# Both ends of a gated state-space convolution kernel rewritten on one core: opening by channel halves, first and last six pairs reordered, no clip

## The chip, the cores and the metric

The kernel runs on one core of a Trainium2 chip. A core has a matrix engine (TensorE, "PE" in the profile, with "PEld" for its weight loads), a vector engine (VectorE, "DVE"), an activation engine (ScalarE, "ACT"), a general engine (GpSimd, "POOL") and a sequencer that only issues transfers here (SyncE, "SP"). Each works through its own instruction list in order and waits on semaphores. The metric is the time of one execution in device microseconds (us); lower is better.

## What is computed

The input x has shape (4, 128, 96, 96). It is group-normalised (32 groups), read as a sequence of 9216 positions in four directions (rows, columns, and both reversed), and each direction runs through the same block:

```python
t = grouped1x1(x, in_proj)                  # 128 -> 512 channels, 4 groups
u, gate = t[:, :256], t[:, 256:]
u = depthwise_conv5(silu(u))
s = ssm_in(u); a = 0.999 + 0.0009 * sigmoid(ssm_delta(u))
a = clip(a, 0.0001, 0.9999)
bb, cc = tanh(ssm_b(u)), tanh(ssm_c(u))     # 32 channels each
h[l] = a[l] * h[l-1] + bb[l] * s[l]         # written as cumsum in the reference
u = u + ssm_out(cc * h + d * s)
y = out_proj(grouped1x1(u * sigmoid(gate), mix))
```

The four results are mixed by a 1x1 convolution (fuse) and added to x. The clip's upper end is the value that `a` has where the sigmoid is 1, so it never moves `a` by more than rounding.

## The kernel before, in words

All arithmetic is float32. A *unit* is one direction of one block of 384 positions; two opposite directions make a *pair*. There are 8 phases (4 images, columns then rows), 6 steps in a phase, 4 pairs in a step: 192 pairs, numbered t = 0 to 191. `R` = 4 sub-sequences, `LAG` = 6.

`pair(t)` (line 762) writes the order of all five engines out by hand (line 916, `manual_schedule`): what stands first in the source is issued first on its engine. In one call it does, for pair t, the depthwise convolution and the projections, and for pair t-6 the rest:

- `front(t+4)` (413, 466): in-projection by 32x32 matmuls out of `x_in`, then four silu on ACT (480) into the tile `sil`. Only in the first three steps of a phase; the others reload `sil` from device memory.
- `conv` and `conv_less` (587, 596): the lower 128 channels' taps as matmuls with the banded weights `band` and `less`; ACT copies the sum to `u` (606, 608). `taps` (613): the upper 128 channels' five taps, the first on ACT (623, `first_tap`), four on DVE (625).
- `proj` (637): 16 matmuls with `main`, then on ACT tanh, copy, tanh (654 to 656), on POOL the decay `a` and its clip (659; for the second and third pair of a step the clip is DVE's, 789) and the product of bb and s (662).
- `scan` (685): two DVE scans for each step, in the first two pairs of the next one. `outputs` (700): two POOL products and a POOL copy for each pair, which make z; `scale_s` (677, 679) on ACT.
- `gates_and_out` or, where gates were kept, `out_of` (494, 497): matmuls from z into the banks 0 to 3, over a copy of u put there by ACT (`under`, 502, 505); `gating` (563, 574) on DVE; `accumulate` (715): 16 matmuls with `w_fin` for each unit, an ACT copy `ys` (727, 729), a POOL add to the image `acc` (743).

PSUM has eight banks. Banks 0 to 3 serve `out_of`, `under` and the taps; in the first six pairs `conv` and `proj` both use banks 4 and 5 (`PROJ`, 120) and `front` 7, 6, 2, 3 (`FRONT`). Transfers are all on SP's queue, in the order of the source: `load_front` (249) fetches `x_in` for a later step as soon as a front has read its part, `keep_silu` (453) writes 770 KB of `sil` to device memory, `load_chunks` (390) fetches pieces of the next image for its statistics.

Ahead of the pairs, not hand ordered: x is loaded and its statistics taken on DVE (281), weights are merged (351 to 369), POOL builds `band` and `less` with 64 scalings of 32 columns (343), and `stats_finish` (175) turns the statistics into scaled weights `wn` (225) and biases `bnorm` (238). The weight-merging tiles lie in a pool that is closed at line 370; `sil` takes over its memory. `fronts` for the first four groups follow (909 to 914).

Behind the pairs, `tail` (869): for the six pairs still open (186 to 191) `out_of`, `gating`, `under`, two scans, `outputs`, `accumulate`, one pair after the other, and the last four transfers of 384 KB to the result.

Of the kernel before, what the change touches and what calls it, by code (L numbers as in the profile page):

```python
# [52 lines left out]
DMIN, DMAX = 0.999, 0.9999  # L53
PAD = K // 2
# [12 lines left out]
def conv_preact_kernel(  # L67
# [214 lines left out]

    b0 = phases[0][0]
    first_table = wp.tile([P, 1], F32, name="first_table")
# [50 lines left out]
    for s in range(2):  # L335
        for p in range(R):
            for k in range(2):
                r, to = slice(0, P), band[:, s, p]
                if k == less_of(p):
                    r, to = less_rows(s, p), less[:, p]  # L340
                for g in range(4):
                    m = R * k - p + R - 1
                    nc.gpsimd.tensor_scalar_mul(  # L343
                        to[r, g, :], id32[r, :], w_dw[r, s, g, m : m + 1]
                    )
# [23 lines left out]
    nc.scalar.activation(b_fin, pb[:, 0:1], AF.Identity, bias=b_fuse)  # L369
    prep.__exit__(None, None, None)  # L370
# [46 lines left out]
    def front_parts(i, banks):  # L417

        step, g = divmod(i, R)
        if step * UB >= NU:  # L420
            return
        st = step % NS
        if st == NS // 2:
            sils[step] = sils[step - 1]
            load_silu(step + 1, (g,))
        elif st == NS - 1 and g < 2:
            load_silu(step, (2 * g, 2 * g + 1))
        elif g == 0 and fresh(step):
            sils[step] = wk.tile([P, 2, 2, 4, N + 1], F32, tag="sil", name=f"sil_{step}")
        if fresh(step):  # L430
            yield from compute_front(step, g, banks)
        sil = sils[step]

        if st == 0:
            engine = nc.gpsimd if step else nc.vector
            for s in range(2):
                engine.memset(sil[64 * s : 64 * s + 64, s, 0, g, 0:1], 0.0)
            if g < 2:
                engine.memset(sil[:, :, 1, g, 0:1], 0.0)

        for s in range(2):
            load_front(step + 1, s, slice(64 * s + 32, 64 * s + 64), slice(g, g + 1))
        if g == R - 1:
            for s in range(2):
                load_front(step + 1, s, slice(64 * s, 64 * s + 32), slice(0, R))
        if st < NS // 2 - 1:
            to_keep.append((step, g))
        if step > 1:
            keep_silu(1)
# [15 lines left out]

    def compute_front(step, g, banks):
        un = units[step * UB]
        wn, bn = stats[un["b"]]
        sil = sils[step]
        for s in range(2):  # L470
            for j in range(2):
                r = slice(64 * s + 32 * j, 64 * s + 32 * j + 32)
                for c in range(4):
                    m, q = (c, g) if j else (g, R - 1 - c if s else c)
                    mm(bank(banks[2 * s + j]), c, wn[r, s, 32 * m : 32 * m + 32],
                       x_in[s][r, q, :], True, True)
        yield
        for s in range(2):
            for j in range(2):
                nc.scalar.activation(  # L480
                    sil[:, s, j, g, :],
                    bank(banks[2 * s + j])[:, : N + 1],
                    AF.Silu,
                    bias=bn[:, 1:2] if j else bn[:, 4 + g : 5 + g],
                )
# [47 lines left out]
    def load_last():  # L533

        t = wk.tile([P, 2, 2, 4, N + 1], F32, tag="sil", name="last_gates")
        for e in range(R):
            n = NU // 2 - R + e
            old_gates[n] = t[:, :, :, e, :N]
            nc.sync.dma_start(old_gates[n], kept[n // NP % 2][mirror(n)])
# [97 lines left out]
    def proj(i, banks, apart=False):  # L637

        step, p = units[i]["step"], units[i]["p"]
        if step not in scans:  # L640
            t0 = wk.tile([P, N, R], F32, tag="t0", name=f"t0_{step}")
            scans[step] = t0.rearrange("p n r -> p r n")
        ta = scans[step]
        tb = tbs[i] = wk.tile([P, N], F32, tag="t1", bufs=LAG + 1, name=f"t1_{units[i]['id']}")

        turns = [(e, j) for j in (1, 0) for e in range(2)]
        for e, j in sorted(turns) if apart else turns:
            for c, cols in enumerate(((qb, qb, qa, qa), (qs, qs, qc, qc))[e]):
                first, end = (j == 0, j == 1) if apart else (j == 1, j == 0)
                mm(bank(banks[e]), c, w_proj[:, j, cols], us[i][:, c % 2, j, :], first, end)  # L650
        pa, pb = (bank(bk)[:, :N] for bk in banks)

        tm = tms[i] = wk.tile([P, N], F32, tag="tm", name=f"tm_{units[i]['id']}")
        nc.scalar.activation(tm, pa, AF.Tanh, bias=b_proj[:, 0:1])  # L654
        nc.scalar.copy(tb[0:64, :], pb[0:64, :])
        nc.scalar.activation(tb[64:P, :], pb[64:P, :], AF.Tanh, bias=b_proj[64:P, 1:2])  # L656
        for op in decay(i):
            if i < NU - 2:
                nc.gpsimd.tensor_scalar(*op)  # L659
            if clip_late(i):  # L660
                break
        nc.gpsimd.tensor_mul(ta[0:64, p, :], tb[0:64, :], tm[0:64, :])  # L662

    def decay(i):

        a = scans[units[i]["step"]][64:P, units[i]["p"], :]
        half = (DMAX - DMIN) / 2
        return (
            (a, tms[i][64:P, :], half, DMIN + half, ALU.mult, ALU.add),
            (a, a, 0.9999, 0.0001, ALU.min, ALU.max),  # L670
        )

    def clip_late(i):

        return units[i]["p"] in (1, 2)
# [24 lines left out]
    def outputs(i, copy=nc.gpsimd.tensor_copy):  # L700
        ta, tb, p = scans[units[i]["step"]], tbs[i], units[i]["p"]
        nc.gpsimd.tensor_mul(ta[0:64, p, :], tb[64:P, :], ta[64:P, p, :])  # L702
        nc.gpsimd.tensor_add(tb[0:64, :], ta[0:64, p, :], tb[0:64, :])  # L703
        copy(tb[64:P, :], tb[0:64, :])
# [10 lines left out]
    def accumulate(bu, bk, adder=nc.gpsimd, last=False):  # L715

        b, s, p, st = bu["b"], bu["s"], bu["p"], bu["st"]
        py = bank(bk)
        for j in range(2):
# [4 lines left out]
        if not (last and s == 1):  # L724
# [17 lines left out]
        def add():  # L742
            adder.tensor_add(part, y, part)  # L743
# [17 lines left out]

    def pair(t):
# [5 lines left out]
        with_front = fresh((t + R) // R)  # L768
        seed = old or back and not with_front

        ahead = old or back and not with_front
        banks, w = plan(with_front or not back)
        if back:
            front(t + R, FRONT)
# [5 lines left out]
        send()  # L780
# [5 lines left out]
        new_u(i)  # L786
        taps(i, range(1, K))
        if t and clip_late(i - 2):
            nc.vector.tensor_scalar(*decay(i - 2)[1])
        conv(i, banks)  # L790
        if not ahead:
            conv_less(i, banks)
        if not back:
            first_tap(i + 2)
            front(t + R, FRONT)
# [14 lines left out]
        if waiting and not late:  # L810
            accumulate(waiting.pop(0), w[0])()
# [6 lines left out]
        if ahead:  # L818
            accumulate(waiting.pop(0), w[1])()
# [33 lines left out]
        proj(i, PROJ, between)  # L853
# [7 lines left out]
        if t == NU // 2 - 3:  # L861
            load_last()
# [6 lines left out]
    def tail():  # L869

        first, banks = NU // 2 - LAG, (6, 7, 4, 5)

        for op in decay(NU - 2):
            nc.vector.tensor_scalar(*op)
        scale_s(NU - 2)
        outputs(2 * first + 2)
        last = None
        for n in range(first, NU // 2):
            i = 2 * n
            for s in range(2):  # L880
                for j in range(2):
                    out_of(i, s, j)
            for s in range(2):
                gating(i, s)
                if i + 2 < NU:
                    under(i + 2, s)
            if n == first:
                for part in range(2):
                    scan(NU // UB - 1, part)

            if last:
                last()
            if i + 4 < NU:
                outputs(i + 4, lambda *_: None)
            accumulate(waiting.pop(0), banks[2])()
            last = accumulate(waiting.pop(0), banks[3], nc.vector)
            if i + 4 < NU:
                nc.scalar.copy(tbs[i + 4][64:P, :], tbs[i + 4][0:64, :])
            send()
            waiting.extend(units[i : i + 2])  # L900
        last()
        for s in range(2):
            accumulate(waiting.pop(0), banks[2 + s], nc.vector, True)()
            send()

    pieces = stats_finish(b0)
    for _ in range(4):
        next(pieces)
    fronts = [front_parts(i, [4 * (i % 2) + e for e in range(4)]) for i in range(R)]
    next(fronts[0])  # L910
    next(pieces, None)
    for parts in fronts:
        for _ in parts:
            pass
    taps(0, range(1))
    with tc.manual_schedule(
# [3 lines left out]
    ):  # L920
        for t in range(NU // 2):
# [81 lines left out]
```

## Time and profile before

| what | value |
|---|---|
| median of 4 runs (lowest to highest) | 1841.81 us (1840.99 to 1843.59) |
| the profiled execution: its own time | 1842.24 us |
| the profiled execution: its span | 1840.5 us |
| busy: PE, ACT, POOL, DVE | 1806.4, 1567.8, 1564.5, 1546.0 us |
| PE busy in 0 to 100 us | 81.20 of 100 us |
| PE busy in 100 to 1775 us | 1669.15 of 1675 us |
| PE busy in 1803.4 to 1840.5 us | 28.12 of 37.1 us |

The profile is a record of one execution: the page sums it up, and the trace behind it can be asked for a stretch of time. In a timeline row the numbers are start, duration, engine, line, operation, output and inputs, shape, count, and in brackets the idle time ahead of it and what ended that. In a row of windows they are, for a stretch of time, the busy time of PE, PEld, DVE, ACT and POOL with instruction counts, the share of full speed that TensorE's clock was granted, the share of time in which the transfer engines worked, and GB/s. One `matmul` of the source is two PE instructions in the count (32 rows x384 are 16 calls).

### The profile page before, as it was taken

How to read it: one execution, taken by the hardware profiler on the slowest of the kernel's cores; microseconds unless marked ns; L12 is line 12 of the kernel's file. 1: busy time of each engine (PE TensorE's matmuls, PEld its weight loads, DVE VectorE, ACT ScalarE, POOL GpSimd, SP SyncE). 2: the span in 40 equal slices, each digit the busy share in tenths (PEclk: the TensorE clock that was granted, in tenths of full speed). 3: DMA queues.
4: the chain of work that ended last, by engine and by line, in shares of the span. 5: the costliest groups of instructions: out<-in, count | busy, mean ns of one | idle time of the engine just before them, and what ended most of it. 6: DMA issues, size and time to landing. Idle time of an engine off the chain costs nothing.

```text
span 1840.5 us, 57440 instructions
## 1 busy us (share of the span) xinstructions
PE 1806.4 (98%) x24024; PEld 650.9 (35%) x24024; DVE 1546.0 (84%) x1541; ACT 1567.8 (85%) x2773; POOL 1564.5 (85%) x1615
## 2 busy tenths in 40 slices
PE   6999999999999999999999999999999999999998
PEld 3233333333333333333333333333333333333332
DVE  5889888888888988988888998888888888788886
ACT  4888888988888888898888888888888888888975
POOL 5489998889878999888887999888888789998886
PEclk7999999999999999999999999999999999999999
DMA  6755464543975467344695556543477634645434
GB/s 195 193 195 179 130 203 118 172 143 130 290 245 177 160 186 212 101 144 139 197 304 202 167 170 197 147 143 117 159 227 230 234 126 136 205 108 177 148 108 168
DMA packets 147826, 321.18 MB, mean 175 GB/s; under 512 B 14192, under 2 KB 115696, under 8 KB 147568
## 3 DMA queue, kind: packets, MB, share of 16 engines
q1 hardware_dynamic: 147136, 316.56, 54.0%
q8 instruction: 189, 3.10, 0.7%
q10 hardware_dynamic: 432, 0.96, 0.1%
q14 instruction: 69, 0.57, 0.1%
HBM read 185.21 MB, written 132.25 MB: 172 GB/s over the span
## 4 chain that ended last, share of the span: by engine, by line
PE 92%; ACT 3%; POOL 2%; issue 1%; DVE 1%; POOLq 0%; DVEq 0%; ACTq 0%
PE psum L133 79%; PE psum L497 8%; PE psum L491 5%; ACT sil L480 1%; ACT psum L623 0%; POOL acc L743 0%; ACT u L606 0%; POOL t L659 0%; POOL t L702 0%; POOL t L703 0%; ACT t L656 0%; ACT tm L654 0%; POOL t L662 0%; ACT t L679 0%; DVE u L574 0%
## 5 line engine op out<-in xcount | busy, mean ns | idle before, releaser
L625 DVE SCALAR_TENSOR_TENSOR psum<-sil,small,psum 128x768 f32<-128x768 f32 x576 | 589.1, 1023 | 35.6 <-ACT psum L623 9.5
L133 PE MATMUL psum<-u,w_fin 128*32 128x384 f32 x6144 | 551.9, 489 | 0.0
L133 PE MATMUL psum<-u,main 128*32 128x384 f32 x6144 | 534.9, 489 | 0.0
L574 DVE SCALAR_TENSOR_TENSOR u<-gate,psum 128x768 f32<-128x768 f32 x376 | 349.6, 952 | 166.9 <-ACT gate L514 85.0
L743 POOL TENSOR_TENSOR acc<-ys,acc 128x384 f32<-128x384 f32 x376 | 414.5, 1123 | 23.8 <-ACT ys L729 5.8
L702 POOL TENSOR_TENSOR t<-t,t 64x384 f32<-64x384 f32 x192 | 256.1, 1334 | 86.6 <-DVE t L696 49.0
L133 PEld LDWEIGHTS psum<-u,w_fin 128*32 128x32 f32 x6144 | 188.1, 110 | 321.0 <-issue 219.1
L133 PEld LDWEIGHTS psum<-u,main 128*32 128x32 f32 x6144 | 181.7, 110 | 326.0 <-issue 199.4
L133 PE MATMUL psum<-sil,band 128*32 128x384 f32 x3072 | 288.8, 491 | 8.1 <-ACT ys L729 3.1
L703 POOL TENSOR_TENSOR t<-t,t 64x384 f32<-64x384 f32 x192 | 283.9, 1478 | 15.1
L505 ACT COPY psum<-u 128x768 f32<-128x768 f32 x352 | 276.8, 800 | 13.0 <-DVE u L625 9.0
L659 POOL TENSOR_SCALAR t<-tm 64x384 f32<-64x384 f32 x191 | 177.7, 930 | 98.3 <-ACT tm L654 68.7
L497 PE MATMUL psum<-t,main 32*128 32x384 f32 x1536 | 241.0, 513 | 3.9 <-POOL t L703 1.5
L623 ACT ACTIVATE psum<-sil,small 128x768 f32<-128x768 f32 x192 | 174.1, 907 | 63.3 <-DVE u L574 56.3
L514 ACT ACTIVATE gate<-psum,bnorm 128x384 f32<-128x384 f32 x384 | 192.6, 581 | 28.8 <-PE psum L491 26.3
L662 POOL TENSOR_TENSOR t<-t,tm 64x384 f32<-64x384 f32 x192 | 201.6, 1050 | 15.3
L625 DVE SCALAR_TENSOR_TENSOR u<-sil,small,psum 128x768 f32<-128x768 f32 x192 | 194.9, 1015 | 7.8
L480 ACT ACTIVATE sil<-psum,bnorm 128x385 f32<-128x385 f32 x384 | 191.6, 584 | 5.5 <-POOL band L343 3.4
L133 PE MATMUL psum<-sil,less 64*32 64x384 f32 x3072 | 168.7, 496 | 0.0
L491 PE MATMUL psum<-x_in,wn 32*128 32x384 f32 x768 | 162.3, 528 | 2.4 <-ACT u L606 1.2
L729 ACT COPY ys<-psum 128x384 f32<-128x384 f32 x287 | 132.9, 476 | 31.0 <-PE psum L133 29.1
L133 PEld LDWEIGHTS psum<-sil,band 128*32 128x32 f32 x3072 | 89.2, 109 | 184.1 <-issue 89.6
(87 smaller groups left out, 1664.3 us busy)
## 6 DMA issues: line engine op xcount, KB each, us to landing
sil<-sil SPq DMA_DIRECT2D x128, 770.0 KB, 6.9
kept<-gate SPq DMA_DIRECT2D x80, 768.0 KB, 3.7
gate<-kept SPq DMA_DIRECT2D x76, 768.0 KB, 6.3
x_in<-in_xs SPq DMA_DIRECT2D x192, 96.2 KB, 2.5
out<-acc SPq DMA_DIRECT2D x48, 384.0 KB, 7.8
acc<-in_xr SPq DMA_DIRECT2D x38, 384.0 KB, 6.7
xs<-in_xr SPq DMA_DIRECT2D x72, 192.0 KB, 4.6
x_in<-in_xs SPq DMA_DIRECT2D x184, 48.1 KB, 4.6
```

The lines of the kernel that those rows point to most:

```text
L133: nc.tensor.matmul(o[r, : rhs.shape[-1]], lhsT, rhs, start=start, stop=stop, skip_group_check=True)
L480: nc.scalar.activation(sil[:, s, j, g, :], bank(banks[2 * s + j])[:, : N + 1], AF.Silu, bias=bn[:, 1:2] if j else bn[:, 4 + g : 5 + g],)
L491: nc.tensor.matmul(bank(to)[:, :N], stats[un["b"]][0][r, s, :], x_in[s][r, q, off : off + N], start=True, stop=True)
L497: nc.tensor.matmul(bank(SSM + 2 * s + j)[:, :N], w_so[r, bass.ts(j, P)], z[r, :], start=bi not in seeded, stop=True, skip_group_check=True)
L505: nc.scalar.copy(psum[:, SSM + 2 * s : SSM + 2 * s + 2, :N], us[bi][:, s])
L514: nc.scalar.activation(gv[:, s, j, :], bank(to[2 * s + j])[:, :N], AF.Tanh, bias=bn[:, 2 + j : 3 + j], scale=0.5,)
L574: nc.vector.scalar_tensor_tensor(v, g, 1.0, pz, ALU.add, ALU.mult)
L625: nc.vector.scalar_tensor_tensor(us[i][:, :, 1, :] if k == K - 1 else part, src, w_tap[:, k : k + 1], part, ALU.mult, ALU.add,)
L662: nc.gpsimd.tensor_mul(ta[0:64, p, :], tb[0:64, :], tm[0:64, :])
L702: nc.gpsimd.tensor_mul(ta[0:64, p, :], tb[64:P, :], ta[64:P, p, :])
L703: nc.gpsimd.tensor_add(tb[0:64, :], ta[0:64, p, :], tb[0:64, :])
L743: adder.tensor_add(part, y, part)
```

## The change

- `band` and `less`: 16 POOL products of 4 x 32 columns, in place of 64 scalings of 32.
- `stay_busy(n)`: a PE matmul of n columns whose result nobody reads, into a bank free at the time. Four of 512 columns behind the weight merging, one of 256 and one of 512 between the steps of `stats_finish`.
- `start()` stands in the hand-ordered part: `stats_finish` to its end, biases included, then the lower channel half (j = 0) of all four fronts, its silus, then the upper half by groups, with pair 0's convolution and taps between them.
- Pairs 0 to 5: `conv` and `proj` use banks 4 and 5 in odd pairs, 6 and 7 in even ones; `front` takes the other two and 2, 3. Pair 0's front(4) stands inside its `proj`.
- The clip of `a` is left out everywhere, and the half range of `a` is 0.00044998 in place of 0.00045 (a change to the computation, of the size of rounding).
- Pairs 188 to 191 and the tail: the kept gates of the last four pairs are loaded one or two at a time; the result's transfers of pairs 190 and 191 wait for the tail; pair 191 adds to `acc` on DVE straight out of PSUM; z of pair 187 is made before pair 191's product; the last decay is ACT's; the tail is a new order, with the unit s = 1 (and some s = 0) added by DVE straight from PSUM, z of pair 188 made on DVE, and pair 191 gated, multiplied, added and sent by halves of 192 positions.

```diff
@@ bands
-                for g in range(4):
-                    m = R * k - p + R - 1
-                    nc.gpsimd.tensor_scalar_mul(
-                        to[r, g, :], id32[r, :], w_dw[r, s, g, m : m + 1]
-                    )
+                nc.gpsimd.tensor_mul(
+                    to[r],
+                    id32[r].unsqueeze(1).broadcast_to(shape),
+                    w_dw[r, s, :, m : m + 1].broadcast_to(shape),
+                )
@@ filler
+    def stay_busy(n):
+        if n:
+            nc.tensor.matmul(
+                bank(free[0] ^ 1)[:, :n], w_fin[:, 0, 0, :],
+                w_fin.rearrange("p d j c -> p (d j c)")[:, :n], start=True, stop=True,
+                skip_group_check=True,
+            )
...
+    for _ in range(4):
+        stay_busy(512)
     prep.__exit__(None, None, None)
@@ opening
+    def start():
+        pieces = stats_finish(b0)
+        for wait in (0, 256, 512, 0, 0):
+            next(pieces, None)
+            stay_busy(wait)
...
+        for g in range(R):
+            burst(0, g)
+        for g in range(R):
+            silus(0, g)
+        new_u(0)
+        for g in range(R):
+            burst(1, g)
+            silus(1, g)
+            after_front(0, g)
+            if g < 2:
+                taps(0, (g,))
+            if g == 1:
+                conv(0, head_banks(0))
+                conv_less(0, head_banks(0))
+        taps(0, (2, 3, 4))
@@ first six pairs
+    def head_banks(t):
+
+        return PROJ if t % 2 or t >= LAG else FRONT[1::-1]
...
+            if i == 0 and (e, j) == (0, 1):
+                front(R, (5, 4, 2, 3))
...
-            front(t + R, FRONT)
+            if t:
+                front(t + R, FRONT if banks == PROJ else (5, 4, 2, 3))
@@ clip
-        for op in decay(i):
-            if i < NU - 2:
-                nc.gpsimd.tensor_scalar(*op)
-            if clip_late(i):
-                break
+        if i < NU - 2:
+            nc.gpsimd.tensor_scalar(*decay(i))
@@ tail, its new order (n is a pair; first = 186, end = 192)
+        z_copy(first + 1)
+        ssm_out(first)
+        gate_units(first)
+        for bk in (4, 5):
+            accumulate(waiting.pop(0), bk)()
+        scan(NU // UB - 1, 0)
+        scale_s(NU - 2)
+        ssm_out(first + 1)
+        gate_units(first + 1)
+        scan(NU // UB - 1, 1)
+        outputs(2 * first + 4, nc.gpsimd.tensor_copy, nc.vector)
+        outputs(2 * first + 6, None)
+        for bk in (6, 7):
+            wait.append(accumulate(waiting.pop(0), bk, nc.vector, True))
+        for n in range(first + 4, end):
+            outputs(2 * n, None)
+        finish(first + 1)
...
+        ssm_out(first + 2)
+        for n in range(first + 2, end - 1):
+            gate_units(n)
+            add()
+            if n > first + 2:
+                finish(n - 1)
+            ssm_out(n + 1)
```

## The prediction

> **What bounds the kernel now.** I read the page first, then PE's busy time by long windows, then short windows and the timeline at both ends.
>
> ```profile
> span 1840.5 us, 57440 instructions
> ...
> PE 1806.4 (98%) x24024; PEld 650.9 (35%) x24024; DVE 1546.0 (84%) x1541; ACT 1567.8 (85%) x2773; POOL 1564.5 (85%) x1615
> ...
> PE 92%; ACT 3%; POOL 2%; issue 1%; DVE 1%; POOLq 0%; DVEq 0%; ACTq 0%
> ```
>
> PE is nearly never idle. Where its 34 us of idle time lie, the long windows tell:
>
> ```profile
> 0.00:100.00 100.00, 81.20 (x1080) 32.94 (x1084) 67.44 (x103) 65.90 (x137) 54.77 (x113) 0.88 0.67 192
> 100.00:1775.00 1675.00, 1669.15 (x22332) 597.79 (x22324) 1431.84 (x1392) 1462.69 (x2574) 1461.43 (x1460) 1.00 0.55 174
> 1775.00:1803.40 28.40, 27.95 (x354) 10.01 (x346) 24.37 (x24) 21.28 (x34) 25.17 (x25) 1.00 0.66 242
> 1803.40:1840.50 37.10, 28.12 (x276) 10.14 (x272) 22.34 (x24) 17.91 (x32) 23.15 (x20) 0.93 0.30 114
> ```
>
> So 1675 us in the middle are PE's own work: the change adds and removes none of it there. The time can only move at the ends, 100 us ahead and 37 us behind. In the opening the clock is a second loss:
>
> ```profile
> 12.40:15.70 3.30, 3.15 (x29) 3.06 (x28) 3.30 (x9) 0.92 (x5) 2.89 (x9) 1.00 1.00 410
> 15.80:19.10 3.30, 0.00 (x0) 0.00 (x0) 3.27 (x8) 0.05 (x1) 2.89 (x10) 0.50 1.08 249
> ...
> 29.40:32.80 3.40, 3.40 (x60) 1.04 (x46) 0.30 (x5) 3.37 (x8) 0.00 (x0) 0.50 0.17 42
> ...
> 36.30:39.60 3.30, 3.30 (x29) 0.70 (x21) 2.04 (x2) 0.01 (x1) 0.00 (x0) 0.50 0.14 50
> 39.70:43.00 3.30, 3.30 (x68) 1.28 (x64) 1.25 (x2) 2.99 (x7) 0.00 (x0) 1.00 0.12 33
> ```
>
> The third number from the end is the clock: 0.50 from 15.8 to 39.6. The rows to keep from the timeline are the start of the silus, one early pair on PE, and the tail's waits:
>
> ```profile
> 27.69 4.83 ACT L480 ACTIVATE sil<-psum,bnorm 128x385 f32<-128x385 f32 x10 [3.38 <-POOL band L343]
> ...
> 74.83 2.79 PE L133 MATMUL psum<-u,main 128*32 128x384 f32 x32
> 77.55 1.03 PE L133 MATMUL psum<-x_in,wn 32*32 32x385 f32 x32
> 78.51 1.50 PE L133 MATMUL psum<-sil,band 128*32 128x384 f32 x16
> 79.94 0.88 PE L133 MATMUL psum<-sil,less 64*32 64x384 f32 x16
> ...
> 1808.69 0.91 PE L497 MATMUL psum<-t,main 32*128 32x384 f32 x2 [1.52 <-POOL t L703]
> 1810.60 1.16 PE L497 MATMUL psum<-t,main 32*128 32x384 f32 x6 [1.01 <-POOL t L704]
> ...
> 1834.32 0.56 DVE L743 TENSOR_TENSOR acc<-psum,acc 128x384 f32<-128x384 f32 x1
> ```
>
> I count the head to tanh of pair t (L654): pair 0 at 43.45, pair 5 at 77.49, and the tail from the end of pair 191's projections, 1803.4.
>
> **Opening, up to pair 0's tanh.** The statistics end at 19.88 with the loads, and nothing in that changes. Silus started at 27.69 because their tile takes over memory that POOL's last band (26.30 to 27.65) still used; the biases were ready at 26.77. Bands: 64 scalings of 0.34 us (1.36 for four) become 16 products. No row has one with 128 columns; POOL's 64x384 product is 1.01 us (L662), so 0.34 is the low end and 1.36, no gain, the high one. Either way they end between 10 and 26, behind DVE's statistics; I take 0.4. The bound is then the biases.
>
> The fillers: 16 calls of 384 columns, four abreast, start 2.72 us of PE work, so a call takes about 0.65 and one of 512 columns 0.86 at full clock, 1.7 at half. Four start at 15.6. With the clock at 0.50 from 15.8 and restored by a full 3.4 us of them, two run slowly and two fast: they end at about 20.9, 0.8 behind the 20.03 at which the first statistics product (L186) ran. If the clock comes back at once they cost nothing; if late, 2.4 us. From there the chain L186 to `wn` took 3.5 us (20.03 to 23.52), of which 1.6 PE at half clock: 2.9 now. Biases (25.21 to 26.56, 1.35 at half clock) follow at once in about 1.2. With hand-overs the first silu starts 4.4 behind 20.9, at 25.3.
>
> Then ACT paces: eight silus of 0.48 to 29.1; conv 1.43 and less 0.86 to 31.4 at full clock; on ACT two silus, first tap 0.9, two silus, u copy 0.8, four silus, to 34.5; DVE's four taps of 1.04, each behind its silu, end at 36.6; next first tap and four silus to 39.4. Beside this, front(4) needs `x_in` rows whose load is issued behind the last burst, at 34.5; such loads took 3.6 us (list of transfers, 192.5 KB): 38.1, half a front 0.5, half a projection 1.4, so about 39.8. Pair 0's tanh is at 39.8 against 43.45: **-3.7 us**. If the clock falls again on the way, conv, less, four bursts and half a projection (6.5 us) double, most of it on the path: about +4, and nothing is won. If neither filler nor load costs anything, 38.3: -5.2.
>
> [...]
>
> **Pairs 1 to 5.** A pair took 6.78 (tanh rows 57.15, 63.93, 70.71): conv waited 0.54 for ACT's reading of the same banks and ran 0.3 slowly. With banks in turn it follows the projections at once. PE's own sum, from the starts above and 80.80: 2.72 + 0.96 + 1.43 + 0.86 = 5.97. ACT: u copy 0.8, first tap 0.85, silus 1.9, tanh, copy, tanh and scale 2.15, 5.7. DVE: taps 4.2, statistics 1.05 or a scan of 1.75 to 2.4, up to 6.6 in two pairs, with slack of 1 us ahead of it. So PE paces: 5 x 5.97 = 29.9 against 34.04. What is late next are loads: `sil` writes of 770 KB (6.9 us median) stand in SP's queue ahead of step 2's rows, and front(8) read at 67.11, with 5.8 us from the front that freed them. Now 5.0 are left: I take 1 us of wait, ends 0 and 2.5. Together **-3.1 us**. If the cover fails in each pair the 6.78 stay, and nothing is won here.
>
> From pair 6 on the order is as before: 9.55 and 10.66 for pairs 6 and 7 stay.
>
> **Middle.** The clip took POOL 0.92 or DVE 0.53 to 1.17 in each pair. PE idles 5.85 us in 1675 there, and its waits name ACT's copies. I take -0.3, with the clip's removal worth 0 at one end and 1 at the other. A loss has no bearer: no instruction is added.
>
> **Pairs 188 to 191.** Projections started 8.67, 8.42, 8.25 apart (1775.30, 1783.97, 1792.39, 1800.64), PE's own being 8.25: 0.6 of waits behind DVE. Without the clip **-0.3**.
>
> **Tail,** in us behind 1803.4. PE's work: six `out_of` of 0.9 and seven pairs' output of 2.7, 24.3; before, the span ended at 37.1. Walking the new order: out_of(186) to 0.95, output(185) to 3.6; out_of(187) waits for ACT's `under` behind DVE's gating(186), to 4.6; output(186), (187) to 10.0. Meanwhile DVE: scan (2.0) to 4.85, gating(187) to 6.7, scan to 8.5, z of pair 188 in two products of 0.6 to 9.7 (no such row on DVE; its adds of 128x384 were 0.55 to 1.2), POOL's copy 0.5. out_of(188) to 11.1. POOL only now begins z of 189, 190, 191, 2.55 each (1.2 + 1.2 and gaps): 12.75, 15.2, 17.75. So PE waits here: out_of(189) is done at 14.75. Then no more waits of size: output(188) to 17.45, out_of(190) 18.7, output(189) 21.4, out_of(191) 22.6, output(190) 25.3, four halves of 0.65 to 27.9. DVE's halves of the sum are added from 26.45 to 28.45. Transfers: before, 6.2 us lay between the add ahead of the first of four transfers (1834.26) and the end. The same four now start at 26.45: 32.7. To it 0.6 for the clock: the window 1807.8 to 1811.1 with 1.41 us of PE lost it, and the new wait between 11.1 and 14.75 may do so again (1.4 us, as outputs took 4.18 there in place of 2.79). 33.3 against 37.1: **-3.8 us**; ends -1.5 (DVE's products at 1.2, POOL blocked, clock lost) and -6.5 (no wait at 11).
>
> **Sum** against the profiled execution: -3.7 - 3.1 - 0.3 - 0.3 - 3.8 = -11.2, 1842.24 to 1831.0. Its time is 0.43 over the median, so 1830.6 for the median; 1830.5 is given.
>
> **Rivals.** (1) *Both covers hold*, no filler delay, no wait for loads, no wait at 11: -5.2 - 4.1 - 0.5 - 6.5 = -16, 1826. For it: most of my waits are under 1 us. (2) *The clock falls in the opening*: +4, 1834.5. For it: the row 29.40 to 32.80; against: fillers are full-array matmuls. (3) *Pairs 1 to 5 stay at 6.78* as loads or DVE pace them: 1834; for it, front(8) was within 0.1 us of its load before. With (2), 1838. (4) *Slower*: PE takes its list in order, so fillers at half clock hold the statistics back to 22.4 and the first silu to 27.2; with bursts, conv and less at half clock the last burst ends at 40.8, its loads land at 45.5, and front and projection, doubled, end at 49.6, 6.2 later than before; and the clock is still at 0.50 when the dense pairs start. Each such pair costs 5.97 more. With -3.1, -3.8 and -0.6 for the rest, the first cold pair decides: none gives 1840.5, one 1846.5, two 1852.5. Against it: conv lifted the clock within 5 us at 39.6. (5) *It doesn't do what it says*: the scheduler could put fillers elsewhere, but PE's new list has them ahead of and between the statistics' products.
>
> **How the numbers follow.** Forecast 0.50 (1828 to 1833.5), rival 1 0.17, rivals 2 and 3 0.27, both 0.03, rival 4 0.03. The range from 1825 to 1836.5 reaches from rival 1's side to just over rivals 2 and 3. A measurement here tells about 0.2%, 3.7 us: faster than 1838.1 by forecast and rivals 1 to 3, 0.94; within, 0.03; slower 0.03.
>
> **What would show it.** First silu at 25 to 25.5 and no POOL wait ahead of it; clock 1.00 from about 19; pair 0's tanh near 39.8, pair 5's near 70.7; 6.0 between pairs, one of 7; 100 to 1775 us shifted and otherwise alike; 33 us behind pair 191's projections, PE idle once for 2 to 3 us in them. Wrong would be: 0.50 in the clock between 20 and 40, a pair interval still at 6.8, or a tail of over 35.

## The result, and the profile after

The changed kernel took 1839.87 us (median of 33 runs, 1834.39 to 1844.69), the kernel before beside it 1842.15 (51 runs, 1840.84 to 1844.44): a ratio of 0.9986, 95% interval 0.9981 to 0.9992. Forecast were 1830.5 and a range of 1825 to 1836.5: the sign was right, the size was not, and the range did not hold it. The profiled execution took 1843.83 us, its span was 1842.1. First the page of the changed kernel: span, busy time, and the shares of the chain that ended last.

```profile
span 1842.1 us, 57282 instructions
...
PE 1813.1 (98%) x24068; PEld 654.7 (36%) x24068; DVE 1451.1 (79%) x1451; ACT 1567.7 (85%) x2762; POOL 1424.0 (77%) x1469
...
PE 95%; ACT 2%; DVE 1%; DMA 1%; issue 0%; SPq 0%; POOL 0%; DVEq 0%; POOLq 0%
```

PE is 6.7 us busier than before, of which its six fillers alone are 6.4 (3.68, 0.68 and 2.06), and transfers are on the chain that ended last (1%), where they were not. Long windows of the changed kernel: start and end, length, busy time of PE, PEld, DVE, ACT and POOL, granted clock, share of the transfer engines, GB/s.

```profile
0.00:100.00 100.00, 84.45 (x1040) 34.63 (x1044) 60.49 (x95) 63.36 (x127) 33.37 (x60) 0.88 0.63 180
100.00:1775.00 1675.00, 1669.17 (x22360) 597.62 (x22352) 1344.42 (x1306) 1466.57 (x2577) 1350.23 (x1371) 1.00 0.55 174
...
1804.90:1842.10 37.20, 30.11 (x307) 11.97 (x304) 21.15 (x28) 15.87 (x26) 15.65 (x15) 0.88 0.47 171
```

In the middle PE is busy as long as before (1669.15 there). The opening's clock is still 0.88, the tail's fell from 0.93 to 0.88. PE's timeline says where (start, duration, operation, and in brackets the idle time ahead and what ended it):

```profile
14.63 3.68 PE L286 MATMUL psum<-w_fin 128*128 128x512 f32 x8
20.04 0.35 PE L187 MATMUL psum<-mv,gmean 128*128 128x1 f32 x2 [1.73 <-DVE mv L184]
...
41.39 2.44 PE L134 MATMUL psum<-x_in,wn 32*32 32x385 f32 x32 [3.24 <-DMA x_in<-in_xs]
43.76 2.79 PE L134 MATMUL psum<-u,main 128*32 128x384 f32 x16
...
69.41 0.88 PE L134 MATMUL psum<-x_in,wn 32*32 32x385 f32 x16 [2.51 <-DMA x_in<-in_xs]
70.81 0.88 PE L134 MATMUL psum<-x_in,wn 32*32 32x385 f32 x16 [0.51 <-DMA x_in<-in_xs]
71.61 4.48 PE L134 MATMUL psum<-u,main 128*32 128x384 f32 x32
...
1819.28 2.79 PE L520 MATMUL psum<-t,main 32*128 32x384 f32 x8 [2.02 <-ACT psum L528]
1822.00 5.02 PE L134 MATMUL psum<-u,w_fin 128*32 128x384 f32 x32
```

PE waits four times: 1.73 ahead of the statistics' product, 3.24 and 3.02 for rows of `x_in`, 2.02 in the tail. Behind the last three stands work that takes up to twice as long: the half projection 2.79 in place of 1.50, the projections of pair 4 4.48 in place of 2.79, an output 5.02 in place of 2.79. Short windows of the same kernel, cut where its clock changes:

```profile
17.50:20.90 3.40, 1.67 (x6) 0.52 (x4) 2.68 (x8) 0.00 (x0) 0.00 (x0) 1.00 1.08 211
...
27.75:31.10 3.35, 3.35 (x64) 1.32 (x48) 0.29 (x5) 2.89 (x7) 0.00 (x0) 0.50 0.00 0
...
38.00:41.30 3.30, 0.15 (x4) 0.00 (x0) 2.27 (x3) 0.92 (x2) 0.00 (x0) 1.00 0.62 149
...
68.70:72.10 3.40, 2.18 (x40) 0.68 (x44) 3.33 (x3) 2.34 (x4) 0.00 (x0) 1.00 1.09 216
...
1816.35:1819.70 3.35, 1.33 (x9) 0.58 (x8) 2.56 (x4) 1.35 (x3) 3.19 (x3) 1.00 0.00 0
1819.75:1823.10 3.35, 3.35 (x16) 1.36 (x18) 1.52 (x2) 1.33 (x2) 3.12 (x4) 0.50 0.02 5
```

The clock was 0.50 from 20.91 to 34.56, 41.39 to 48.22, 72.11 to 75.53 and 1819.73 to 1826.56 (and from 1840.21, behind PE's last work): 13.65, 6.83, 3.41 and 6.83 us, all multiples of 3.41. Ahead of each fall stand 3.4 us in which PE was idle for a third of the time or more (busy for 1.67, 0.15, 2.18 and 1.33 us in the rows above). By stages, from tanh to tanh (L683 after, L654 before):

| stage | before | forecast | changed kernel | lean version (below) |
|---|---|---|---|---|
| start to pair 0's tanh | 43.45 | 39.8 | 45.34 | 41.16 |
| pairs 1 to 5 | 34.04 | 30.9 | 36.39 | 29.48 |
| pair 5's tanh to pair 191's | 1725.93 | 1725.3 | 1723.19 | 1723.26 |
| from there to the end | 37.1 | 33.3 | 37.2 | 34.2 |

Its 33 runs are no cloud about one time. In 17 the granted clock was 0.993 or less, and they took 1839.87 to 1844.69; in 16 it was 0.994 or more, 1834.39 to 1839.02. Time multiplied by clock gives 1825.2 to 1829.8 in all 33.

### The profile page after: what moved, and what is told of

Its sections match the earlier page's. It is cut to its first block, busy times and chain, and to the rows that moved or that the text cites. A ratio compares the mean times of both kernels' runs of the same rounds, so it can differ in the third digit from the quotient of the medians.

```text
span 1842.1 us, 57282 instructions
## 1 busy us (share of the span) xinstructions
PE 1813.1 (98%) x24068; PEld 654.7 (36%) x24068; DVE 1451.1 (79%) x1451; ACT 1567.7 (85%) x2762; POOL 1424.0 (77%) x1469
## 4 chain that ended last, share of the span: by engine, by line
PE 95%; ACT 2%; DVE 1%; DMA 1%; issue 0%; SPq 0%; POOL 0%; DVEq 0%; POOLq 0%
PE psum L134 81%; PE psum L520 8%; PE psum L514 5%; DMA x_in<-in_xs 1%; DVE bn L282 1%; ACT sil L495 0%; DMA acc<-in_xr 0%; DMA xs<-in_xr 0%; DVE u L600 0%; ACT t L701 0%; ACT t L689 0%; ACT psum L649 0%; DVE psum L651 0%; ACT t L684 0%; ACT u L632 0%
## 5 line engine op out<-in xcount | busy, mean ns | idle before, releaser
L724 POOL TENSOR_TENSOR t<-t,t 64x384 f32<-64x384 f32 x191 | 236.2, 1237 | 156.7 <-PE psum L514 79.0
L725 POOL TENSOR_TENSOR t<-t,t 64x384 f32<-64x384 f32 x191 | 246.8, 1292 | 15.0
L692 POOL TENSOR_TENSOR t<-t,tm 64x384 f32<-64x384 f32 x192 | 195.1, 1016 | 15.4 <-ACT t L684 0.2
```

The source lines that it names most:

```text
L724: engine.tensor_mul(ta[0:64, p, :], tb[64:P, :], ta[64:P, p, :])
L725: engine.tensor_add(tb[0:64, :], ta[0:64, p, :], tb[0:64, :])
```

## The experiments

**Theory:** the order does what was forecast, but its waits, two of them for loads, are followed by half clock (0.50 for 3.41 to 13.65 us in the trace above), and that costs more than the waits. **Rivals:** the new order itself gains nothing and only the clip's removal does; or another engine sets the pace. Kernels of one group ran on one chip, and the rows stand by groups: four groups of four, one of two. Each kernel has 5 to 11 runs; ratios are to the kernel before beside them (1842.35 to 1843.09). The last three columns are of one traced run each.

| kernel | median (range), us | ratio, 95% | pair 0's tanh | pairs 1 to 5 | tail |
|---|---|---|---|---|---|
| noclip | 1840.65 (1839.10 to 1841.38) | 0.9985 (0.9976 to 0.9994) | 42.93 | 34.05 | 37.3 |
| tail_alone | 1838.81 (1837.93 to 1840.55) | 0.9977 (0.9968 to 0.9986) | 43.68 | 34.06 | 37.2 |
| head_alone | 1835.34 (1833.80 to 1839.60) | 0.9960 (0.9948 to 0.9972) | 39.30 | 33.04 | 36.6 |
| tail_fill | 1833.48 (1832.32 to 1837.80) | 0.9952 (0.9940 to 0.9965) | 40.04 | 36.73 | 34.2 |
| early_rows | 1831.68 (1831.18 to 1837.61) | 0.9939 (0.9925 to 0.9953) | 43.15 | 32.73 | 36.7 |
| more_fillers | 1840.71 (1836.77 to 1842.50) | 0.9987 (0.9978 to 0.9996) | 43.06 | 34.82 | 36.7 |
| rows_writes | 1831.67 (1828.68 to 1834.89) | 0.9938 (0.9925 to 0.9950) | 38.84 | 29.66 | 37.3 |
| all_four | 1829.76 (1829.34 to 1833.02) | 0.9933 (0.9920 to 0.9945) | 40.60 | 29.50 | 34.2 |
| lean | 1828.01 (1827.17 to 1829.94) | 0.9922 (0.9910 to 0.9935) | 41.16 | 29.48 | 34.2 |
| fillers_off | 1840.86 (1838.38 to 1843.56) | 0.9991 (0.9983 to 1.0000) | 45.25 | 31.61 | 36.7 |
| before_filled | 1840.85 (1839.28 to 1841.68) | 0.9988 (0.9980 to 0.9997) | 44.92 | 34.04 | 36.2 |
| fill_32 | 1835.22 (1833.64 to 1840.39) | 0.9964 (0.9952 to 0.9976) | 39.54 | 34.43 | 35.9 |
| after_again | 1834.30 (1831.06 to 1837.11) | 0.9954 (0.9941 to 0.9968) | 41.67 | 31.06 | 36.7 |
| fill_only | 1834.09 (1833.28 to 1835.30) | 0.9954 (0.9942 to 0.9967) | 41.13 | 34.94 | 34.2 |
| lean_late_writes | 1833.21 (1828.16 to 1835.10) | 0.9945 (0.9932 to 0.9957) | 42.11 | 32.90 | 34.2 |
| lean_no_tail_fill | 1831.33 (1829.33 to 1832.29) | 0.9937 (0.9925 to 0.9950) | 38.70 | 29.55 | 37.1 |
| after_third | 1834.98 (1834.31 to 1840.17) | 0.9963 (0.9951 to 0.9976) | 39.91 | 34.07 | 36.6 |
| lean_again | 1829.84 (1827.13 to 1830.88) | 0.9926 (0.9912 to 0.9939) | 41.33 | 29.60 | 34.2 |

### The change in parts: noclip, tail_alone, head_alone

noclip is the kernel before with the clip's lines out; tail_alone adds the new tail to it, head_alone the new opening and first pairs.

> The kernel before with the clip alone left out, as in the changed kernel. Theory (the clip's removal is what is left of the gain): 2 to 3 us below before, 1839.5, with the distance from pair 5's tanh to pair 191's at about 1723.2 where before had 1725.9. Rival (the middle's 2.7 us are owed to the pairs' other start, not to the clip): no difference from before, 1842.

> The kernel before without the clip and with the new tail; opening and pairs 1 to 5 as before. Theory (a wait of PE of about 2 us in the new tail costs the clock of the next two 3.4-us windows, and that loss eats what the new order gains): from the projections of pair 191 to the end 37 us again, the clock at 0.50 for about 6.8 us in it, and a time of 1839.5, some 2.5 below before, all of it from the clip. Rival (the tail's own order gains 3.8 as forecast, and only the opening went wrong): a tail of 33 to 34 and a time near 1835.5.

> The changed kernel with the tail of before (without the clip). Theory (PE's waits in the new opening and in pairs 1 to 5 cost the clock, and differently from run to run): pair 0's tanh between 40 and 45.5, pair 5's between 72 and 82, a time of 1836 to 1843 with a spread of 8 us or more over its runs, the later the lower the granted clock of the run. Rival (the spread comes from the tail): a spread of 3 us as before, and a time of 1841.

The clip's removal alone gave 2.3 us, within what the theory asked for. They arise at four places: pairs 24, 72, 120 and 168 are the first of the phases by rows, and their interval fell from between 10.40 and 10.47 to 9.33, with 0.46 given back in the next pair. The tail alone has a median 1.8 lower still, where the theory said 0 and the rival 3.8. But in its trace the tail is 37.2 with 0.50 for 6.8 us in it, as the theory had it and as long as noclip's (37.3), and at a granted clock of 0.991 both kernels' runs took about the same (1839.62 to 1841.38 and 1839.80 to 1840.55): the 1.8 goes with the clock, and its trace shows no shorter tail. The head alone gave 5.3 on noclip, with a spread of 5.8 us where noclip has 2.3; the late run is the one with the low clock (0.992 against 0.995 to 0.997). So the order gains in the opening and in pairs 1 to 5 (39.30 and 33.04 in the trace, 42.93 and 34.05 in noclip's), and the rival "only the clip" falls. The three parts add up to 9.4 us; the changed kernel gained 2.3 in its first session, and in its two later sessions (below) it was 8.05 and 8.11.

### The tail's clock: tail_fill, fill_32

```diff
         ssm_out(first + 2)
+        free[0] = 7
+        for _ in range(2):
+            stay_busy(512)
```

> The changed kernel with two more filler matmuls of 512 columns in the tail, behind out_of of pair 188, where PE waited 2.02 us. They compute nothing that is read. Theory (the clock, not the order, made the tail 37.2): the clock stays at 1.00 through 1826, out_of of 189 takes 0.93 in place of 2.79 and the output behind it 2.8 in place of 5.0, the tail is 33.1 to 33.6 and the time 3.5 to 4 below that of the changed kernel. Rival (the walk itself is late, the chain through VectorE and ScalarE sets the tail): PE waits elsewhere for what it gains, tail 36 to 37.5, no gain or up to 0.5 us lost to the fillers.

Timeline of PE, kernel tail_fill, at that place:

```profile
1812.21 1.98 PE L286 MATMUL psum<-w_fin 128*128 128x512 f32 x4
1814.30 2.06 PE L520 MATMUL psum<-t,main 32*128 32x384 f32 x8
1816.29 2.79 PE L134 MATMUL psum<-u,w_fin 128*32 128x384 f32 x32
```

The fillers take the place of the wait, the output behind them is back at 2.79, the tail at 34.2 (37.2): 3.0 us won by two products that nobody reads. It is 34.2 in all six kernels of the table that have them and 36.6 to 37.3 in those whose new tail leaves the wait open. The chain of the rival, ACT's copy ahead of `out_of`, is there too: 2.06 in place of the 0.93 that the theory had, and so 34.2 and not 33.1 to 33.6. The median, 1833.48, is 6.4 under the changed kernel's first session and 0.8 and 1.5 under its later ones; 3.5 to 4 had been expected, and no session has the two beside each other.

fill_32 fills the same wait with `mm(bank(6), c, w_fin[0:32, 0, 0, 32*c : 32*c+32], ...)` for c in 0 to 3, twice: 32 of the array's 128 rows.

> The changed kernel with its tail's wait filled not by two full-array matmuls of 512 columns but by two rounds of four 32x32 matmuls of 512 columns side by side, of the same length, in a quarter of the array. They compute nothing that is read. Theory (the clock goes by the work of the array in a window, not by the time in which PE has an instruction): PE is busy through the wait, and the clock still falls behind it: 0.50 for one or two windows from about 1812 to 1822, tail 36 to 37.5, no gain on the changed kernel. Rival (any instruction on PE counts): clock 1.00 as with the full-array fillers, tail 33.5 to 34.3.

Timeline, then windows of fill_32:

```profile
1809.58 1.92 PE L134 MATMUL psum<-w_fin 32*32 32x512 f32 x16
1811.66 2.06 PE L520 MATMUL psum<-t,main 32*128 32x384 f32 x8 [0.17 <-ACT psum L528]
1813.65 4.48 PE L134 MATMUL psum<-u,w_fin 128*32 128x384 f32 x32
```

```profile
1810.60:1814.00 3.40, 3.23 (x25) 1.04 (x17) 2.37 (x4) 2.01 (x3) 3.17 (x4) 1.00 0.03 5
1814.00:1817.40 3.40, 3.40 (x28) 1.29 (x24) 0.96 (x2) 2.52 (x4) 3.32 (x4) 0.50 0.01 2
```

PE is busy for 3.23 of 3.40 us and the clock still falls behind it; the output takes 4.48. The tail is 35.9, a hair under what the theory expected: the clock was 0.50 for 3.4 us, and for 6.8 behind the changed kernel's wait. Busy time alone does not hold the clock in this trace.

### Loads: early_rows, rows_writes, lean_late_writes

```diff
         for g in range(R):
             burst(0, g)
+        for s in range(2):
+            load_front(1, s, slice(64 * s, 64 * s + 32), slice(0, R))
```

> The changed kernel with four loads issued earlier: the rows of x_in of step 1 that the first channel half reads are loaded right behind the first half's last burst and not behind the second half's. Theory (that load is what front(4) waited 3.24 us for, and the idle PE behind it lost the clock at 41.4): front(4) starts at about 38.2 without a wait, pair 0's tanh near 41, pair 1's interval 6 to 6.5 and no 0.50 between 41 and 48; 4 to 6 us below the changed kernel. Rival (the clock that the opening loses at 20.9 is lost again whatever the load does): pair 0's tanh at 41 to 42, but 0.50 again before pair 1's projections, 1 to 2.5 us gained.

front(4) ran at 38.12 without a wait, though bursts and convolution were at half clock up to 34.57; no 0.50 followed up to 65. Pair 0's tanh came at 43.15, two later than expected, and pair 1's interval was 5.22, under the 6 to 6.5. The kernel is 2.6 to 8.2 us under the changed kernel, by which of that kernel's sessions one takes. Pair 4 still waited 1.74 us, and behind the wait its projections took 3.95 in place of 2.79.

rows_writes also lets `keep_silu` write at the end of groups 2 and 3 of the opening and in pairs 0 and 1:

```diff
+            keep_silu(g // 2)
...
-        keep_silu((1, 2, 1, 0)[t] if t < R else 0)
+        keep_silu((1, 1, 0, 0)[t] if t < R else 0)
```

> As the kernel with the early rows, and the four writes of step 0's silus (770 KB each) issued earlier too, two within the opening, one each in pairs 0 and 1. Theory (front(8) waits in pair 4 for rows queued behind those writes, and the clock falls behind the wait): pair 4's interval 6 in place of 10.6, no 0.50 near 72 to 75, pair 5's tanh 3 to 5 us nearer to pair 0's than in the kernel with the early rows alone. Rival (the rows are late for the transfers' own length, 6 to 7 us from issue, not for the queue): pair 4 still waits 2 us or more. Second rival (writes in the opening hold up the rows of step 1): pairs 1 to 3 wait instead.

Pair 4's interval fell from 9.71 to 6.62, its wait to 0.53, and pairs 1 to 5 took 29.66, under the forecast's 30.9. In the medians the two kernels are equal (1831.68, 1831.67), which the traces do not explain: the traced run of early_rows was its slowest (1837.61), and its four others took 1831.18 to 1832.73. So the writes were put back late in the lean version below:

> The lean version with the four writes of step 0's silus where the changed kernel had them. Theory (front(8) then waits some 2.5 us for rows behind these writes and its clock falls): pair 4's interval 9 to 10.6, and 2.5 to 4 us above the lean version. Rival (with the clock held up to there the wait is all): 2.5 at most, pair 4 at 8.5 to 9.

Pair 4's interval is 9.82 and the median 5.2 us above lean in another group, 3.4 above lean_again: by one measure more than the theory's range, by the other within it. Its trace, however, also has 0.50 from 24.26 to 34.50 in the opening, ahead of these writes, and one of its five runs, at a clock of 1.000, took 1828.16, as lean does. So the late writes hold front(8) up (it waited 2.04, 0.40 in lean), but what a run pays for it is mostly clock.

### Fillers in the opening: fillers_off, more_fillers, before_filled

fillers_off takes out the change's own six; more_fillers has five more, two of them ahead of the first two bursts of the second half, and so ahead of the convolution; before_filled has them in the order of before without the clip.

> The changed kernel with its own six filler matmuls left out. Theory (they run at 14.6 to 18.3, a window too early, and keep the clock in some phases of the windows only): 0.50 from 14 or 18 to 34 in every run, as before's opening, first silu 26.3 to 26.8, pair 0's tanh 45 to 46 and a time of 1841 to 1845 without the runs at 1834 to 1836. Rival (the fillers do nothing either way): median and spread as with them, 1834 to 1845 about 1839.9.

> The changed kernel with five more filler matmuls of 512 columns in the opening: six in place of four ahead of the statistics, two in place of one ahead of the biases, one ahead of each of the second half's first two bursts. Theory (the clock falls where a 3.4-us window has PE idle for half of it): 1.00 from about 11 to 38, the first silu still at 26.3 or up to 0.7 earlier, the six bursts at 4 in place of 7 us, the last silu of pair 0 at 35 in place of 38; front(4) then waits for the same load, and pair 0's tanh is at 41 to 42; 2.5 to 4 us below the changed kernel, less if the clock falls again in the wait for the load. Rival (a clock of 0.50 here is no matter of PE's idle time, but of the 32x32 bursts, or is granted late after any load): 0.50 again from 21 or 24 to 34, and the fillers at half clock cost 1 to 2 us.

> The kernel before without the clip and in its own order, with fillers where PE idled: six of 512 ahead of the statistics, 256, 512 and 512 between their products, one each ahead of fronts 2 and 3, two ahead of the convolution, two in the tail behind pair 185's output. Theory (clock and order each have their share): clock 1.00 from about 11 to the end of the tail, first silu still 27.7 behind POOL's bands, pair 0's tanh 40.5 to 41, pairs still 6.78, tail 35.5, together 4 to 4.5 below the kernel before without the clip, 1836; the new order's own share would then be 8 us when loads and clock are kept. Rival (the clock is the whole of it, the order next to nothing): 1831 or less. Second rival (fillers at half clock hold the statistics up): 1841 or more.

Without its fillers the changed kernel has no run under 1838.38 and a clock of 0.990 to 0.992 in all (its median, 1840.86, is a hair under what was expected); fill_32, which keeps them, has five of six runs at 1833.64 to 1837.85 in the same group. So the changed kernel's runs at 1834 to 1838 are owed to them, and the rival that they do nothing falls. more_fillers missed: with five more the clock was 1.00 from 9.34 to 40.06, as the theory had it, and the kernel was no faster all the same. The fillers among the bursts put the convolution at 30.40, where rows_writes had 27.12; front(4) came at 38.97 only, behind a wait of 3.39, and the clock fell behind it and behind pair 4's wait. A filler costs what it delays: with the same fillers, early rows and early writes, all_four has pair 0's tanh 1.8 later than rows_writes. before_filled missed: its clock fell at 27.85 among its bursts, fillers at half clock held up the silus, pair 0's tanh came 2.0 later than in noclip, and the tail's 1.1 us made up for half of it; the medians are equal (1840.85, 1840.65). So this kernel does not tell what the clock alone would give to the old order; its pairs stay at 6.78 at full clock, which is the order's share.

### All together: all_four, lean, lean_again

> The changed kernel with early rows, early writes, the five fillers of the opening and the two of the tail together. Theory (the order gains what was forecast once loads and clock are kept): first silu 25.6 to 26.3, pair 0's tanh 38 to 39.5, pairs 1 to 5 at 6 to 6.3 each, pair 5's tanh at 69 to 70.5, a tail of 33.3, clock 1.00 throughout, and a time of 1825 to 1828 with a spread under 3 us. Rival (another limit stands behind, ScalarE or VectorE in the opening and in pairs 1 to 5): pair 0's tanh at 41 or later, pairs at 6.7, and 1831 or more.

The clock was 1.00 from 10.17 to 1826.06 and the pairs took 29.50, as expected; pair 0's tanh at 40.60 and the tail of 34.2 are later than that by 1 us each, the median by 2, with a spread of 3.7 where under 3 was expected. lean has the early rows, the early writes and the tail's fillers as above, and drops the fillers among the second half's bursts (which its expectation calls the first half's):

```diff
-    for _ in range(4):
+    for _ in range(6):
         stay_busy(512)
...
             if i == 0 and (e, j) == (0, 1):
+                stay_busy(512, 5)
                 front(R, (5, 4, 2, 3))
```

> The changed kernel with early rows, early writes and the two fillers of the tail, as the one with all four, but fillers in the opening only where PE idles anyway: six of 512 ahead of the statistics, one ahead of the biases, none among the first half's bursts, one ahead of front(4). Theory (the order holds its forecast when loads and clock are kept, and the fillers among the bursts cost 1.8 us of pair 0): first silu 24.3, pair 0's tanh 38.9, pairs 1 to 5 29.7, tail 34.2, 1827 to 1828.5 if the clock is kept. Rival (the fillers among the bursts are what kept the clock): 0.50 again somewhere between 23 and 40 and 1830 or more.

Timeline of PE, kernel lean:

```profile
12.89 1.84 PE L379 MATMUL psum<-small,w_of 128*128 128x1 f32 x16
...
15.49 7.09 PE L286 MATMUL psum<-w_fin 128*128 128x512 f32 x12
22.42 0.28 PE L187 MATMUL psum<-mv,gmean 128*128 128x1 f32 x2
...
38.42 1.50 PE L134 MATMUL psum<-u,main 128*32 128x384 f32 x16 [0.30 <-DVE u L651]
...
61.42 0.88 PE L134 MATMUL psum<-x_in,wn 32*32 32x385 f32 x16 [0.40 <-DMA x_in<-in_xs]
```

Its median is the lowest of all, 14.7 us under the kernel before (lean_again, 13.25 under, is level with all_four, 12.9), and it kept its clock from 19.24 on. The first silu was missed (26.63, expected 24.3): the clock had fallen at 15.82, behind the weight merging's matmuls of one column, the six fillers ran half of their 7.09 us at half speed, and L187 came at 22.42, not 20; pair 0's tanh is at 41.16, not 38.9. Even so the median was within what was expected.

### The shares on one chip: after_again, fill_only, lean_no_tail_fill, after_third

> The changed kernel once more, unchanged, beside the next three. Theory (its time is that of its order, some 1827 to 1828 with the loads' waits of 4 to 5 us in it, plus the clock lost in that run, and which windows fall is a matter of how the 3.4-us grid lies): a spread of 8 us or more again between about 1834 and 1844.5, each run's time higher the lower its granted clock; pair 4 waits for x_in in its trace whatever the clock does. Rival (a part of the spread is the chip): another median here, and the same within it, spread under 4 us.

> The changed kernel with the fillers of the lean version (six ahead of the statistics, one ahead of front(4), two in the tail), its loads and writes as they were. Theory (clock and loads each cost, and the waits for loads bring a part of the clock's loss): front(4) and front(8) wait as before, 0.50 behind each of these waits, tail 34.2; 1831 to 1834. Rival (the fillers alone hold the clock and that is the whole loss): 1829 or less.

> The lean version without the two fillers of the tail. Theory (0.50 for 6.8 us behind PE's wait in the tail, in most places of the grid): tail 37 to 37.5 in place of 34.2, and 2.5 to 3.5 us above the lean version. Rival (the tail's clock cost more in the kernel with these fillers alone, by chance of the opening's grid, or less): no more than 1 us.

> The changed kernel a third time, unchanged, on one chip with the lean version. Theory (its time is its order's plus the clock that a run loses): a median anywhere from 1834 to 1840 with a spread of 6 to 10 us, each run's time by its granted clock, 5 us or more above the lean version. Rival (the lean version's 1828 was that chip's and not the kernel's): the two within 3 us of each other.

> The lean version once more. Theory: 1827 to 1830 with a spread of 3 us or less and a granted clock of 0.999 or over, whatever the chip. Rival (its steadiness was chance): a spread of 5 us and a median over 1830.5.

The changed kernel unchanged took 1834.30 and 1834.98 in two further sessions, 4.9 to 5.6 less than in the first, while the kernel before moved by 0.9: both theory and rival of after_again have a part, its spread (6.1 us) goes with the clock (0.994 to 0.998), and its median goes with the session. What makes a session's runs keep or lose the clock stays open. On one chip lean_again was 5.1 us under after_third (1829.84 and 1834.98), with a spread of 3.8 against 5.9, where 3 had been expected. Fillers alone left the median where it was (1834.09 beside 1834.30) and narrowed the spread (2.0 beside 6.1): they held the tail and the clock behind front(4), but pair 4 waited and had 0.50 for 6.8 us behind it (its interval 10.42). Leaving the tail's fillers out cost 3.3 against lean in another group and 1.5 against lean_again, under the 2.5 to 3.5 expected, at a tail of 37.1.

## Why the prediction was wrong

The forecast said 1830.5 and the first session 1839.87, but a part of the distance is luck. The account below is of the traced run, one of the 17 late ones. In the two other traced runs of the changed kernel the opening was 41.67 and 39.91 (39.8 forecast), pairs 1 to 5 31.06 and 34.07 (30.9), the tail 36.7 and 36.6 (33.3), and the medians of those sessions, 1834.30 and 1834.98, lie inside the range that was given. Only the tail's term failed in all three.

**Opening, -3.7; measured +1.9.** The first silu came at 26.30 (25.3 forecast), without POOL's wait. The step that failed is that the fillers "end at about 20.9": it took the clock's fall at 15.8 from one execution of before. Here the clock was full, so they were done at 18.31, left 1.73 us open, and behind the stretch 17.50 to 20.91, in which PE was busy for 1.67 us, the clock was 0.50 for 13.65 us. That 3.4 us of fillers restore a lost clock, as that step has it, this run does not show; lean does (0.50 from 15.82, under its fillers, to 19.24). The price of such a fall had been named (+4, rival 2). What that rival stood on, the row 29.40 to 32.80 (32x32 matmuls, PE busy for all 3.40 us, clock 0.50), held: here too 32x32 bursts filled 27.75 to 31.10 (busy for 3.35 of 3.35 us), and the clock stayed at 0.50 up to 34.56. The load for front(4), issued when the half-speed bursts were done (37.86 in place of 34.5), landed at 41.26 in place of 38.1.

**Pairs 1 to 5, -3.1; measured +2.4.** PE's sum was right: 5.59 and 5.88 where nothing disturbs, 29.5 to 29.7 for all five with loads and clock kept. The failed term is "1 us of wait, ends 0 and 2.5" for front(8): it waited 3.0 (1.1 in after_again, 1.6 in after_third), and 1.7 for the clock came on top. Pair 1 took 7.88, 1.9 more than the sum, at the half clock behind front(4)'s wait.

**Middle, -0.3; measured -2.8**, of which noclip has 2.4. The failed step is that the middle is "PE's own work: the change adds and removes none of it", read from 1669.15 us busy of 1675; the term was then taken from the 5.85 us left, as if spread over all pairs. The gain came from the four phase starts by rows. There the same 32 matmuls took 1.49 to 1.56 us in before and 0.95 in noclip, and no idle time was counted (before, then noclip, pair 24):

```profile
252.41 1.49 PE L133 MATMUL psum<-x_in,wn 32*32 32x385 f32 x32
...
251.90 0.95 PE L134 MATMUL psum<-x_in,wn 32*32 32x385 f32 x32
```

**Pairs 188 to 191, -0.3; measured 0.** 34.22 in place of 34.17.

**Tail, -3.8; measured +0.1.** The failed term is "0.6 for the clock": it was 3.0, the 37.2 of this run against 34.2 with the clock kept. The walk without its clock term, 32.7, was 1.5 short. It had the place of PE's wait (12.3 to 14.4 us behind pair 191's tanh, inside the 11.1 to 14.75 of the forecast), but not what ended it: POOL's z of pair 189 was ready at 1818.81, and ACT's copy `under`, behind DVE's gating of pair 188, at 1819.13.

**The chances** failed in one more step: rivals 2 and 3 had 0.27 together and 0.03 for both, about what two independent chances would give. They share a cause, a wait of PE with half clock behind it (13.65 us behind the wait of 1.73, 3.41 behind that of 3.02). In this profile rival 2 came, and of rival 3 its ground, the load for front(8), though not its pace: four intervals were 5.59 to 7.88 and one 10.62.

So the clock, and with it the time, did not follow from how long PE was busy: it fell behind stretches of 3.4 us with PE busy for 1.67 and 2.18 us, in fill_32 for 3.23, and the 33 runs spread over 10 us.

## What to carry over

Price a wait of TensorE not at its length but with the half-speed work behind it: here a wait of 2.0 us in the tail cost 3.0 us more behind it. Where one kernel's runs differ in their granted clock (0.990 to 0.996 in the 33 here), forecast a spread and not a time. Fill such a wait with full-array products that delay nothing (here two of 512 columns took the tail from 37.2 to 34.2 us), and issue each load behind the last reader of what it overwrites, ahead of the big writes on its queue. Where two rivals have the same cause, give their chance together.

## What the runs showed of the hardware

In these traces the clock does not go by PE's busy time alone. Windows of noclip, ahead of and behind its clock's first fall:

```profile
11.20:14.50 3.30, 3.30 (x33) 3.30 (x31) 3.30 (x8) 1.52 (x7) 2.88 (x9) 1.00 1.02 419
14.60:17.90 3.30, 0.77 (x5) 0.69 (x4) 3.30 (x8) 0.26 (x1) 3.13 (x10) 0.50 1.04 316
```

The first is filled, for the most part, by matmuls with one column and by weight loads (PE and PEld busy for 3.30 of 3.30 us each), and the clock falls behind it at 14.56; so it did in lean (12.41 to 15.82). Full-array products held it with 1.49 of 3.40 us (after_third, 16.20 to 19.60), so the rule in more_fillers' theory, PE idle for half a window, does not hold. The changed kernel's own trace has both: behind 17.50 to 20.90, with 1.67 us busy, the clock fell, and behind 65.30 to 68.70, with 1.60 us busy, it stayed at 1.00 up to 72.11. At 0.50 it stayed there through 24.35 to 31.10, filled by 32x32 bursts, and was 1.00 again behind 31.20 to 34.50, filled for the most part by the convolution (busy for 3.30 of 3.30 us). The same bursts held a clock of 1.00 through 26.10 to 29.40 in lean, where 96 of their matmuls take 3.85 us in place of 6.99.

The runs that set work against busy time are fill_32 and tail_fill. In the same place two rounds of 32x32 products (1.92 us) and two full-array products (1.98 us) stand; behind the first the clock fell and the tail was 35.9, behind the second it stayed at 1.00 and the tail was 34.2. How much work in how long a stretch holds the clock, no run shows.
